# A Mamba and expert-layer kernel: another order for the end of the last chunk, expert weights gathered in four parts, expert chunks in a written order

## The chip, the cores and the metric

The kernel runs on one core of one Trainium2 chip. The metric is the device time of one execution in microseconds (us); the time of a kernel is the median of its runs. The core has five engines that run side by side: TensorE (PE, matrix products; PEld is its loading of weights), VectorE (DVE), ScalarE (ACT), GpSimd (POOL) and SyncE (SP, which here only issues DMAs). Each engine works through its own list of instructions in order and waits on semaphores for the others.

## What is computed

The input is one image of 64 x 64 positions with 256 channels, float32. Two layers are applied, each with residuals:

```
# layer 0
x = x + conv_attention(group_norm(x, 32 groups))
#   1x1, 3x3 and 5x5 convolutions give q, k, v; depthwise 3x3; 8 heads;
#   softmax attention over the 4096 positions; 1x1 projection
# layer 1, t = the 4096 tokens of 256 channels
n = layer_norm(t)
m = mamba_forward(n) + mamba_backward(n)     # inner width 512, state 16, scan over 4096 tokens
h = layer_norm(m) * ln_g + ln_b
t = t + m + leaky_relu(h @ w1.T + b1, 0.01) @ w2.T + b2
# mixture of 8 experts (256 -> 512 -> 256) on n = layer_norm(t)
logits = mean(n, tokens) @ Wr + br           # one routing for the whole sample
two experts by weight -> top_i, softmax of their weights -> top_w
y = sum_k top_w[k] * (gelu(n @ W1[e_k] + b1[e_k]) @ W2[e_k] + b2[e_k])
t = t + layer_norm(y + n) * gamma + beta
```

As the routing hangs on the mean over all tokens, no expert's weights can be fetched before the last token has left the Mamba stage.

## The kernel before, in words

The program has four phases, one behind the other: `conv_phase`, `attention_phase`, `mamba_phase` and `expert_phase`. The tokens are worked in 8 chunks (`NCH`) of 512 tokens (`N`). A tile of a chunk is 128 partitions x 2 x 512: the 256 channels lie in `CT` = 2 groups on the partitions, the tokens in the free direction. A mean over channels is therefore a matmul with the constant `mean_mat`. `P` is 128, `FT` is 4 (512 inner channels by 128).

**The Mamba phase.** Its loop runs over 512 slots: 16 passes (8 chunks forward, 8 backward) of 32 slots. In each slot `recur` issues on DVE one scan over 128 x 1024 elements (L1907, 2.35 us) and one product with C (L1912, 1.22 us), while ACT makes the decays (L1884) and POOL the inputs dbx (L1894) of slots to come. The order of the instructions on every engine is written out by hand: the whole loop stands in `tc.manual_schedule(engines=ORDERED)`, so an engine gets its instructions in the order in which the Python code makes them. Other work is dealt into the slots as generators, piece by piece: each `yield` ends a piece, and `step` runs a generator to its next `yield`.

- `tail(c)` (L1539) is the work on a finished chunk: LayerNorm of `m` (`layer_norm`, L101 to L150, its last product L149 on POOL), the leaky-ReLU MLP, the residual, the LayerNorm whose result goes to `u2d` in HBM, and the sum over tokens `usum` (L1583) that the routing needs. It has 39 pieces, one dealt per slot (L2039). With one piece per slot the tail of chunk 6 does not end within the last pass: its rest is drained in `ending()`.
- `ahead()` (L1687) prepares the end of the last chunk within the last pass. It makes `wc` and the two 128 x 128 matrices `near` and `far`, by which the last output projection is made with its mean taken off, and `b1p` and `b1c` (L1709 to L1714): the bias of the MLP with `ln_b` folded in, and 0.01 times that.
- `ending()` (L1768) finishes the last chunk: the last parts of the projections (`plain`, L1735; `close`), the LayerNorm by small matmuls (`rstd_of`: sums of squares of 128 tokens each into one column, then a power on POOL; `spread`: the four values per partition laid on diagonals, L1763, and spread over the partitions by a matmul, L1766), up projections with leaky ReLU (L1809 to L1811), down projections (L1820), the last residual, the LayerNorm of the expert layer, scores and `router()` (L2045).

`router` leaves `rows_of` (L2065), the rows of the two chosen experts in HBM, and `tw` (L2082), their two weights. Its scratch (`slab`) lies in the tile `win`, which lies where later the gathered weights go.

**The expert phase.** Four indirect DMAs on POOL's queue (L2105) gather the two experts' weights, two halves of a row of 2054 floats for each partition: W1, W2, b1, b2. DVE scales W2 by the expert's weight and takes its mean over channels off (L2113 to L2125). Then for each chunk: load `u` (normed tokens) and `x` (residual) on SP's queue (L2137, L2139), eight groups of two up matmuls with a gelu on ACT each (L2165, L2168), sixteen down matmuls (L2175), `r` = their sum plus bias plus `u` (L2179). A float32 matmul of 512 columns stands in the trace as two records of 0.429 us at full clock. `finish(c)` normalizes `r` while the next chunk runs, one piece behind each gelu: Square (L131), the two matmuls of the sum of squares (L122), four small DMAs with POOL's power between them, product (L149), gamma and beta (L2150), residual (L2153), store (L2154). The last chunk uses `fast_norm` (L154 to L179), in the manner of `rstd_of` and `spread`. This phase stands outside the written order: the framework's scheduler places the instructions. `pmm`, `po` and `pln` are the PSUM pools of the up matmuls, the down matmuls (two buffers) and the LayerNorms.

## Time and profile before

| what | value |
|---|---|
| median of 3 runs | 4116.2 us (4112.8, 4116.2, 4122.62) |
| the profiled execution | 4114.68 us, span 4112.9 us, mean granted clock 0.919 |
| busy: PE, DVE, ACT, POOL | 87%, 85%, 65%, 45% of the span |
| last pass of the Mamba phase | to about 3806 us |
| `ending()` and router | 3806 to 3850 us |
| first gather issued, first up matmul | 3851.05, 3859.03 us |
| experts, one chunk | 29.17 us, 68 PE records |
| last chunk's first matmul | 4065.07 us |
| last down matmul, last store issued | about 4094.4, 4106.47 us |

Times count from the start of the span, so a place in the program is named by its microsecond. A line of the timeline has start, duration, engine, line of the kernel, operation, result and operands, shape, and, where the engine stood idle just before, for how long and what released it. The granted clock is the share of TensorE's full speed that the throttle let through: at 0.5 a matmul record takes twice as long.

### The profile page before, as it was taken

The page shows a single profiled execution, that of the slowest core. Times are in us where ns is not written, and L with a number is a line of the kernel's source. Part 1 is how long each engine was busy: PE and PEld are TensorE (multiplying, and loading weights), DVE is VectorE, ACT ScalarE, POOL GpSimd, SP SyncE. Part 2 cuts the span into 40 slices and gives each one's busy share as a digit, 9 for nine tenths or more (in the row PEclk, how much of TensorE's full clock was granted, in tenths as well). Part 3 has the DMA queues.
Part 4 walks back from the last instruction along what each step waited for, and adds up shares of the span by engine and source line. Part 5 has one row for each costly group of instructions (what it writes and reads, how often), then busy time and mean ns, then how long its engine had stood idle before and what let it go on. Part 6 is the DMA issues. An engine that isn't in the chain of part 4 may idle for free. (4 is left out here: it accounts for less than half of the span.)

```text
span 4112.9 us, 43197 instructions
## 1 busy us (share of the span) xinstructions
PE 3584.9 (87%) x14772; PEld 1175.0 (29%) x14772; DVE 3499.8 (85%) x2908; ACT 2666.2 (65%) x4146; POOL 1839.2 (45%) x1283
## 2 busy tenths in 40 slices
PE   6769888999999999997888888888888888876898
PEld 2324332222222222222222222222222222222343
DVE  8998877989888888877899999999999999999211
ACT  1111226988887888875777778778787778775222
POOL 3020000000000000002888889888888989987000
PEclk9889998999999999998888988998989899988899
DMA  6222215223322322214333344343433334432221
GB/s 208 93 98 96 81 58 157 52 60 65 66 62 55 65 63 57 58 39 138 116 103 121 114 137 139 101 141 106 135 106 127 121 124 120 132 118 80 75 68 35
DMA packets 164051, 399.92 MB, mean 97 GB/s; under 512 B 36981, under 2 KB 45941, under 8 KB 163566
## 3 DMA queue, kind: packets, MB, share of 16 engines
q1 hardware_dynamic: 139198, 312.65, 24.0%
q0 software_dynamic: 24624, 84.43, 8.8%
q8 instruction: 118, 1.93, 0.2%
q14 instruction: 111, 0.91, 0.1%
HBM read 268.16 MB, written 79.56 MB: 85 GB/s over the span
## 5 line engine op out<-in xcount | busy, mean ns | idle before, releaser
L1894 POOL TENSOR_TENSOR dbx<-dtxr,b 128x1024 f32<-128x1024 f32 x512 | 1203.7, 2362 | 197.3 <-DMA dtxr<-dtd 91.3
L1046 ACT ACTIVATE e<-sc 128x1024 f32<-128x1024 f32 x1024 | 993.7, 1023 | 172.0 <-PE sc L1039 147.1
L1907 DVE TENSOR_TENSOR_SCAN da<-da,state,dbx 128x1024 f32<-128x1024 f32 x432 | 1013.9, 2347 | 14.6 <-ACT da L1884 7.2
L956 DVE TENSOR_TENSOR s<-s,e 128x1024 f32<-128x1024 f32 x768 | 880.4, 1216 | 25.0 <-ACT e L1046 24.3
L1884 ACT ACTIVATE da<-dtr,aneg 128x512 f32<-128x512 f32 x1024 | 708.0, 691 | 32.6 <-DMA dtr<-dtd 3.1
L1039 PE MATMUL sc<-q,kS 32*128 32x512 f32 x4096 | 651.9, 648 | 18.6 <-ACT e L1046 13.9
L1912 DVE TENSOR_TENSOR h<-da,c 128x1024 f32<-128x1024 f32 x432 | 529.1, 1225 | 33.1 <-PE y L1947 1.3
L963 PE MATMUL av<-e,vT 128*32 128x512 f32 x4096 | 553.6, 611 | 0.0
L979 POOL DMA_DIRECT2D s<-s x94 | 81.6, 879 | 946.5 <-DVE s L956 856.1
L1947 PE MATMUL y<-h,sel 128*32 128x512 f32 x2048 | 376.1, 664 | 91.6 <-DVE h L1912 66.4
L464 PE MATMUL cv<-v,u 128*128 128x512 f32 x928 | 414.6, 607 | 28.8 <-DVE v L288 13.3
L1039 PEld LDWEIGHTS sc<-q,kS 32*128 32x128 f32 x4096 | 211.4, 185 | 460.7 <-issue 253.1
L1341 PE MATMUL mm<-u,win 128*128 128x512 f32 x464 | 253.6, 697 | 77.6 <-ACT z L1448 25.8
L464 PEld LDWEIGHTS cv<-v,u 128*128 128x128 f32 x928 | 179.4, 195 | 261.7 <-issue 227.8
L562 DVE SCALAR_TENSOR_TENSOR acc<-pad,wdw_s,acc 128x768 f32<-128x768 f32 (+1 forms) x192 | 236.0, 1234 | 19.9 <-ACT acc L555 14.2
L1938 ACT COPY state<-da 128x2 f32<-128x2 f32 x431 | 67.9, 158 | 265.6 <-DVE h L1912 264.7
L143 POOL TENSOR_TENSOR ln_few<-ln_few,minus_half 128x4 f32<-128x4 f32 x29 | 37.4, 1291 | 400.5 <-DMA ln_few<-ln_row 265.4
L1387 PE MATMUL mm<-xp,taps 128*128 128x512 f32 x480 | 213.0, 596 | 0.1
L956 DVE TENSOR_TENSOR s<-e 128x1024 f32<-128x1024 f32 x128 | 151.9, 1217 | 59.5 <-ACT e L1046 59.3
L1907 DVE TENSOR_TENSOR_SCAN h<-da,state,dbx 128x1024 f32<-128x1024 f32 x80 | 187.5, 2344 | 10.6 <-ACT state L1938 9.9
L963 PEld LDWEIGHTS av<-e,vT 128*32 128x32 f32 x4096 | 81.4, 108 | 397.0 <-issue 389.2
L1917 POOL TENSOR_TENSOR h<-h,c 128x1024 f32<-128x1024 f32 x80 | 188.6, 2357 | 1.0 <-ACT state L1938 1.0
(382 smaller groups left out, 3922.1 us busy)
## 6 DMA issues: line engine op xcount, KB each, us to landing
dtr<-dtd SPq DMA_DIRECT2D x128, 512.0 KB
dtxr<-dtd SPq DMA_DIRECT2D x128, 512.0 KB
s<-s POOLq DMA_DIRECT2D x94, 512.0 KB, 6.0
b<-bcd SPq DMA_DIRECT2D x64, 256.0 KB
c<-bcd SPq DMA_DIRECT2D x64, 256.0 KB
dtd<-dt SPq DMA_DIRECT2D x64, 256.0 KB
dtd<-few SPq DMA_DIRECT2D x64, 256.0 KB
u<-uv SPq DMA_DIRECT2D x24, 640.0 KB
```

What stands on the lines that cost most here:

```text
L464: nc.tensor.matmul(rows4(ps), u[:, dy, P * ci : P * ci + P], v[:, dy : dy + HR, ci, :], start=dy + ci == 0, stop=dy == k - 1 and ci == CT - 1,
L562: nc.vector.scalar_tensor_tensor(o, src, w_ap, o, ALU.mult, ALU.add)
L956: nc.vector.tensor_tensor(z, x, y, ALU.add)
L963: nc.tensor.matmul(g.av[32 * h : 32 * h + 32, :], vT[:, kb, P * t + 32 * h : P * t + 32 * h + 32], es[h // 2][:, h % 2, :], start=kb == 0, ...
L1039: nc.tensor.matmul(ps[h // 2][:, h % 2, :], kS[r, t, P * kb : P * kb + P], q_t[r, t, :], start=True, stop=True,)
L1046: nc.scalar.activation(e, ps[i], AF.Exp)
L1341: nc.tensor.matmul(ps, win[d][:, t, P * e : P * e + P], u[:, t, ::-1] if d else u[:, t, :], start=t == 0, stop=t == CT - 1,)
L1884: nc.scalar.activation(da[:, v, :], dts[i, e, j][0][:, v, :], AF.Exp, scale=aneg[i % 2][:, a : a + 1])
L1894: nc.gpsimd.tensor_tensor(u, dts[i, e, j][1], bcs[i, k][0][:, None, :].to_broadcast([P, 2, N]), ALU.mult)
L1907: nc.vector.tensor_tensor_scan(das[n].rearrange("p v n -> p (v n)"), da.rearrange("p v n -> p (v n)"), u.rearrange("p v n -> p (v n)"), st ...
L1912: nc.vector.tensor_tensor(h, da, bcs[i, k][1][:, None, :].to_broadcast([P, 2, N]), ALU.mult)
L1947: nc.tensor.matmul(ys[i, e][32 * j : 32 * j + 32, :], cx.sel, hs[n + j // 2][:, j % 2, :], start=False, stop=k == SQ - 1,)
```

## The change

- `fast_norm` goes. In its place two small functions serve both the end of the Mamba phase and the last expert chunk: `deviations` (sums of squares, reading, power) and `spread` (diagonals and their matmul). Both can work on a part of the columns.
- `ahead()` yields between the small matmuls of `b1p` and their DVE readers; slot 17 joins the list of slots in which `ahead()` gets a step.
- In slots 4, 6 and 7 of the last pass two tail pieces are dealt in place of one.
- `ending()`: Square ahead of the copy; the deviations get a PSUM tile of their own; the spread comes before the rest of the tail is drained; all four up projections come before the first down projection; of the scores only the first pair of matmuls comes before the deviations; the scratch of the router moves to another pool; the store of `u2` goes to ACT's queue.
- The row of an expert's weights becomes W1, b1 | W2, b2, padding (two halves of 1028 floats). Four separate tiles are gathered, in the order W1 and b1 of both experts, then W2 and b2 of both. The gathers then wait for `rows_of` and no longer for `tw`.
- The first `u` is loaded on SP's queue ahead of the gathers. Each chunk's `x` and the next chunk's `u` are issued on ACT's queue behind the fourth gelu.
- The chunk loop stands in the written order. The LayerNorms of chunks 0 to 6 are called with `halves=True`: DVE adds the two channel groups first, and one matmul sums.
- `last_chunk` works the last chunk's down projections in four quarters (two halves of 256 columns, two channel groups) and normalizes and stores each half by itself; beta is added to `x` on ACT.

```diff
-EXPERT_ROW = 2 * FF + 4 * C + FT + CT
+EXPERT_ROW = 2 * (2 * FF + FT)
...
+def deviations(cx, few, ps, sq, cols=range(N // P)):
+    nc, at = cx.nc, slice(cols[0], cols[-1] + 1)
+    for j in cols:
         for t in range(CT):
             nc.tensor.matmul(
-                ps[:, j : j + 1], dst[:, t, P * j : P * j + P], cx.mean_mat[:, 0:1], start=t == 0, stop=t == CT - 1
+                ps[:, j : j + 1], sq[:, t, P * j : P * j + P], cx.mean_mat[:, 0:1], start=t == 0, stop=t == CT - 1
             )
-    nc.scalar.activation(few, ps[:, 0 : N // P], AF.Identity, bias=cx.eps)
-    nc.gpsimd.tensor_tensor(few, few, cx.minus_half, ALU.pow)
-    diag = pool.tile([P, N], FP, name="ln_rstd", tag="ln_rstd", bufs=1)
-    for j in range(N // P):
-        nc.vector.tensor_scalar(diag[:, P * j : P * j + P], cx.ident, few[:, j : j + 1], float(C), ALU.mult, ALU.mult)
-    ps = new_psum()
-    nc.tensor.matmul(ps, cx.mean_mat, diag, start=True, stop=True)
-    nc.vector.tensor_tensor(dst, xc, ps[:, None, :].to_broadcast([P, CT, N]), ALU.mult)
+    nc.scalar.activation(few[:, at], ps[:, at], AF.Identity, bias=cx.eps)
+    nc.gpsimd.tensor_tensor(few[:, at], few[:, at], cx.minus_half[:, at], ALU.pow)
+def spread(cx, ps, diag, few, cols=range(N // P)):
+    for j in cols:
+        cx.nc.vector.tensor_scalar(
+            diag[:, P * j : P * j + P], cx.ident, few[:, j : j + 1], float(C), ALU.mult, ALU.mult
+        )
+    at = slice(P * cols[0], P * cols[-1] + P)
+    cx.nc.tensor.matmul(ps[:, at], cx.mean_mat, diag[:, at], start=True, stop=True)
...
+            yield
             nc.vector.tensor_tensor(b1p, ps[:, 0:FT], cx.col("b1", 0, FT), ALU.add)
             nc.vector.tensor_scalar(b1c, b1p, 0.01, None, ALU.mult)
...
+                nc.scalar.activation(sq[:, co, :], centred[co], AF.Square)
                 nc.vector.tensor_copy(xc[:, co, :], centred[co])
-                nc.scalar.activation(sq[:, co, :], centred[co], AF.Square)
             plain(1, 1)
             few = tl.tile([P, N // P], FP, name="ln_few", tag="ln_few")
-            rstd_of(few, wide[:, 1, :], sq)
+            deviations(cx, few, mm_psum(), sq)
...
             plain(1, 2, 3)
             plain(0, 3)
-            for t in tails:
-                drain(t)
-            spread(wide[:, 1, :], few)
+            rs = mm_psum()
+            spread(cx, rs, bcp.tile([P, N], FP, name="diag", tag="b"), few)
...
+            for t in tails:
+                drain(t)
             pair = pda.tile([P, 2, N], FP, name="pv", tag="da")
-            halves = []
-            for f in range(FT):
-                if f % 2 == 0:
-                    a = tl.tile([P, 2, N], FP, name="a1a", tag=("ln_xc", "a1b")[f // 2])
-                    halves.append(a)
-                pv = mm_psum() if f < 2 else pair[:, f - 2, :]
+            pv = [None] * FT
+            halves = [tl.tile([P, 2, N], FP, name="a1a", tag=tag) for tag in ("ln_xc", "a1b")]
+            def up_proj(f):
...
+            for f in range(2):
+                up_proj(f)
+                leaky(f)
+            for f in range(2, FT):
+                up_proj(f)
+            for f in range(2):
+                down_proj(f)
+            for f in range(2, FT):
+                leaky(f)
+            for f in range(2, FT):
+                down_proj(f)
...
+            score(0)
             few2 = tl.tile([P, N // P], FP, name="ln_few", tag="ln_few")
-            rstd_of(few2, pz, u2)
+            deviations(cx, few2, mm_psum(), u2)
+            for j in range(1, N // P):
+                score(j)
+            slab_of[0], used[0] = up.tile([P, 2, N], FP, name="slab", tag="dbx")[:, 0, :], 0
...
+            nc.scalar.dma_start(out=u2d[c], in_=u2)
+        end, used, slab_of = {}, [2 * P], [win[0][:, 1, :]]
...
-                if i == 2 * NCH - 1 and at in (4, 5, 6, 7, 10, 11, 12, 13, 15, 19, 21, 23, 25, 27, 28, 29, 30):
+                if i == 2 * NCH - 1 and at in (4, 5, 6, 7, 10, 11, 12, 13, 15, 17, 19, 21, 23, 25, 27, 28, 29, 30):
                     last = last or ahead()
                     step(last)
-                if tails and (i == 2 * NCH - 1 or at not in FULL[needs[0]]):
-                    needs[0] = next(tails[0], None)
-                    if needs[0] is None:
-                        tails.pop(0)
-                        needs[0] = "PE"
+                for _ in range(1 + (i == 2 * NCH - 1 and at in (4, 6, 7))):
+                    if tails and (i == 2 * NCH - 1 or at not in FULL[needs[0]]):
+                        needs[0] = next(tails[0], None)
+                        if needs[0] is None:
+                            tails.pop(0)
+                            needs[0] = "PE"
...
+        def load(c, queue):
+            u = io.tile([P, CT, N], FP, name="u", tag="u")
+            queue.dma_start(out=u, in_=u2d[c])
+            return u
         tw = cx.tw
-        HALF = EXPERT_ROW // 2
-        w1s, w2s, b1s = [], [], []
-        b2s = one.tile([P, CT], FP, name="b2s")
-        for k in range(2):
-            ew = one.tile([P, EXPERT_ROW], FP, name=f"ew{k}")
-            for h in range(2):
+        u_next = load(0, nc.sync)
+        ew = [[one.tile([P, EXPERT_ROW // 2], FP, name=f"ew{k}{h}") for h in range(2)] for k in range(2)]
+        for h in range(2):
+            for k in range(2):
                 nc.gpsimd.indirect_dma_start(
-                    out=ew[:, HALF * h : HALF * h + HALF], out_offset=None,
-                    in_=experts.rearrange("r (h c) -> (r h) c", h=2),
+                    out=ew[k][h], out_offset=None, in_=experts.rearrange("r (h c) -> (r h) c", h=2),
                     in_offset=bass.IndirectOffsetOnAxis(ap=cx.rows_of[:, k, h : h + 1], axis=0),
                 )
-            a, b, c = 2 * FF, 2 * FF + 4 * C, 2 * FF + 4 * C + FT
+        w1s = [ew[k][0][:, 0 : 2 * FF].rearrange("p (t f) -> p t f", t=CT) for k in range(2)]
+        b1s = [ew[k][0][:, 2 * FF : 2 * FF + FT] for k in range(2)]
+        w2s, b2s = [], one.tile([P, CT], FP, name="b2s")
...
-            new = lambda: pln.tile([P, N], FP, name="ln", tag="ln")
-            if c < NCH - 1:
-                yield from layer_norm(cx, tl, new, r, o, centred=True)
-            else:
-                fast_norm(cx, tl, new, r, o, centred=True)
+            yield from layer_norm(
+                cx, tl, lambda: pln.tile([P, N], FP, name="ln", tag="ln"), r, o, centred=True, halves=True
+            )
...
+        def last_chunk(u, x, h):
+            c, both = NCH - 1, (range(0, N // P // 2), range(N // P // 2, N // P))
             r = tl.tile([P, CT, N], FP, name="r", tag="r")
+            sq = io.tile([P, CT, N], FP, name="sq", tag="u")
+            o = io.tile([P, CT, N], FP, name="o", tag="o")
+            few = tl.tile([P, N // P], FP, name="ln_few", tag="ln_few", bufs=1)
+            diag = tl.tile([P, N], FP, name="diag", tag="ln_rstd", bufs=1)
+            stat = [pln.tile([P, N], FP, name="ln", tag="ln") for _ in range(2)]
+            for t in range(CT):
+                nc.scalar.activation(x[:, t, :], x[:, t, :], AF.Identity, bias=cx.col("beta", t))
+            def part(half, co):
+                cols = slice(P * half[0], P * half[-1] + P)
+                ps = po.tile([P, N], FP, name="o", tag="o")[:, 0 : N // 2]
+                down_proj(ps, co, h, cols)
+                nc.vector.scalar_tensor_tensor(
+                    r[:, co, cols], ps, b2s[:, co : co + 1], u[:, co, cols], ALU.add, ALU.add
+                )
+                nc.scalar.activation(sq[:, co, cols], r[:, co, cols], AF.Square)
+            def write(half):
+                cols = slice(P * half[0], P * half[-1] + P)
+                for t in range(CT):
+                    nc.vector.scalar_tensor_tensor(
+                        o[:, t, cols], r[:, t, cols], cx.col("gamma", t), stat[1][:, cols], ALU.mult, ALU.mult
+                    )
+                nc.vector.tensor_tensor(o[:, :, cols], o[:, :, cols], x[:, :, cols], ALU.add)
+                nc.sync.dma_start(
+                    out=outT[:, N * c + cols.start : N * c + cols.stop].rearrange("(t p) n -> p t n", p=P),
+                    in_=o[:, :, cols],
+                )
             for co in range(CT):
-                ps = po.tile([P, N], FP, name="o", tag="o")
+                part(both[0], co)
+            part(both[1], 0)
+            deviations(cx, few, stat[0], sq, both[0])
+            part(both[1], 1)
+            spread(cx, stat[1], diag, few, both[0])
+            deviations(cx, few, stat[0], sq, both[1])
+            write(both[0])
+            spread(cx, stat[1], diag, few, both[1])
+            write(both[1])
+        behind = None
+        with tc.manual_schedule(engines=ORDERED):
+            for c in range(NCH):
+                u, h = u_next, hp.tile([P, 2, FT, N], FP, name="h", tag="h")
                 for k in range(2):
                     for f in range(FT):
-                        nc.tensor.matmul(
-                            ps, w2s[k][:, f, P * co : P * co + P], h[:, k, f, :],
-                            start=k + f == 0, stop=k == 1 and f == FT - 1,
-                        )
-                nc.vector.scalar_tensor_tensor(
-                    r[:, co, :], ps, b2s[:, co : co + 1], u[:, co, :], ALU.add, ALU.add
-                )
-            drain(behind)
-            behind = finish(c, r, x)
-        drain(behind)
+                        ps = pmm.tile([P, N], FP, name="mm", tag="mm")
+                        for t in range(CT):
+                            nc.tensor.matmul(
+                                ps, w1s[k][:, t, P * f : P * f + P], u[:, t, :], start=t == 0, stop=t == CT - 1
+                            )
+                        nc.scalar.activation(h[:, k, f, :], ps, AF.Gelu, bias=b1s[k][:, f : f + 1])
+                        step(behind)
+                    if k == 0:
+                        x = io.tile([P, CT, N], FP, name="x", tag="x")
+                        nc.scalar.dma_start(out=x, in_=x2d[c])
+                        if c < NCH - 1:
+                            u_next = load(c + 1, nc.scalar)
+                drain(behind)
+                if c == NCH - 1:
+                    last_chunk(u, x, h)
+                    break
+                r = tl.tile([P, CT, N], FP, name="r", tag="r")
+                for co in range(CT):
+                    ps = po.tile([P, N], FP, name="o", tag="o")
+                    down_proj(ps, co, h, slice(0, N))
+                    nc.vector.scalar_tensor_tensor(
+                        r[:, co, :], ps, b2s[:, co : co + 1], u[:, co, :], ALU.add, ALU.add
+                    )
+                behind = finish(c, r, x)
```

## The prediction

> **What bounds the kernel now.** I read the page's busy shares and its forty slices first, then the stretches after 3700 us, where the edits lie, by windows, and inside them by the timeline with its releasers.
>
> ```profile
> span 4112.9 us, 43197 instructions
> PE 3584.9 (87%) x14772; PEld 1175.0 (29%) x14772; DVE 3499.8 (85%) x2908; ACT 2666.2 (65%) x4146; POOL 1839.2 (45%) x1283
> ...
> 3840.00:3860.00 20.00, 7.72 (x37) 5.50 (x37) 4.56 (x23) 2.53 (x6) 4.95 (x5) 0.58 0.43 146
> 3880.00:3900.00 20.00, 20.00 (x48) 8.89 (x47) 1.50 (x2) 4.37 (x6) 0.00 (x0) 1.00 0.08 26
> ```
>
> The windows' columns are PE, PEld, DVE, ACT and POOL busy, granted clock, DMA share, GB/s. The shares are averages over stages that differ: in the last Mamba pass (to about 3806) DVE runs scan behind scan and every us on it counts. From 3807 to 3867 nothing is full; a chain of waits sets the time, mostly at half clock. In the experts PE is full, and nothing but fewer matmul records helps. From 4094.4 a chain again.
>
> ```profile
> 3744.07 0.16 DVE L1713 TENSOR_TENSOR win<-mm,small 128x4 f32<-128x4 f32 x1 [1.35 <-PE mm L1709]
> 3744.27 0.98 DVE L1714 TENSOR_SCALAR b1c<-win 128x4 f32<-128x4 f32 x1
> 3764.28 0.99 PE L1571 MATMUL tl<-a1a,w2s 128*128 128x512 f32 x1 [2.36 <-DVE m L1576]
> 3815.99 1.22 DVE L1583 TENSOR_REDUCE usum<-u 128x2 f32<-128x1024 f32 x1 [6.18 <-POOL u L149]
> 3817.12 0.86 DVE L1763 TENSOR_SCALAR diag<-ident,ln_few 128x128 f32<-128x128 f32 x4
> 3827.04 1.98 PE L1809 MATMUL pv<-hn_end,w1s 128*128 128x512 f32 x4 [1.56 <-DVE a1a L1811]
> 3851.05 1.09 POOL L2105 DMA_INDIRECT ew<-in_experts,rows_of  x1 [6.80 <-DVE diag L1763]
> 3866.11 0.75 DVE L2113 TENSOR_SCALAR w2k<-ew,tw 128x1024 f32<-128x1024 f32 x1 [1.71 <-DMA ew<-in_experts,rows_of]
> 4070.22 1.88 PE L122 MATMUL ln<-o,mean_mat 128*128 128x512 f32 x4
> 4072.19 0.68 ACT L136 ACTIVATE ln_rstd<-ln,eps 1x512 f32<-1x512 f32 x1 [1.08 <-PE ln L122]
> 4082.51 1.22 DVE L149 TENSOR_TENSOR o<-r,ln_rstd 128x1024 f32<-128x1024 f32 x1 [16.48 <-DMA ln_rstd<-ln_inv]
> 4105.22 1.22 DVE L2153 TENSOR_TENSOR o<-o,x 128x1024 f32<-128x1024 f32 x1
> ```
>
> To be seen: DVE stops for b1p in the last pass; the diagonals (pow of `few` done at 3813.65) stand 3.5 us behind the reduce of tail(6); the gathers wait for DVE and the fourth, landing at 3866.05, holds up PE; each expert LayerNorm costs PE four records.
>
> **The change, part by part.** Line numbers are those of before. Gains are positive.
>
> (1) *Last pass.* The new yield puts a slot (some 3.6 us) between the 16 small matmuls and their DVE reader, so the 1.35 stall goes, and of the 0.98 all but the 0.16 of its neighbour: +2.17. The doubled slots let tail(6) finish inside the pass, so L1583 (1.22) comes before the last scan, on a full DVE: -1.22. POOL's `hn` (3711.44, 2.36) and its ACT readers come a slot earlier among the dbx and decay instructions that feed the scans; no row shows what that does. Bounds: nothing (the pieces before were all absorbed) and three slots at 0.69, the stall of DVE at 3770.70, so -2.1. I take 0, since neither engine is full (dbx 2.36 and decay 1.42 in 3.6). Part: +0.95 (-1.1 to +2.2).
>
> (2) *ending() to `rows_of`.* Square ahead of the copy: 3808.98 becomes 3808.25, +0.73. `few` no longer shares the tile of the plain sums, which waited from 3812.21 to 3812.61: +0.40. The diagonals no longer wait for L1583, but the spread (3818.04) then waits for PE's plain records, done at 3816.99 and now at 3815.9: together about +2.1 from this stretch. All up matmuls before the first down: the 1.56 stall and its weight load go, +1.65. Six of the eight score matmuls go behind the deviations, which started at 3840.88 though their Square had ended at 3839.91: +0.85 of these 0.97, as two scores stay ahead. Sum +4.6, with the pass +5.5 (low 3, high 6.8). What is late next: PE at half clock.
>
> (3) *Gathers.* They waited for the last write of `tw` (ends 3850.11) and now for `rows_of` (3848.23): +1.88, so the first is issued at S = 3851.05 - 5.5 - 1.9 = 3843.6. Before, it landed 7.85 later and the fourth 11.1 after its issue, while six u and x loads (3.1 MB) and 2.1 MB of gathers filled the DMA engines from 3852 to 3866. Now one u load has come before, the others are issued after the fourth gelu. Landing without company: the page's other 512 KB transfers on POOL's queue take 6.0. Upper bound as before (7.85, 11.1), lower 4.3 for the first (1.09 issue, 1.3 us of 526 KB at 410 GB/s, and 2 us of latency, an estimate from the 128 KB row's 2.5). I take 6.0: first at S+6.0, fourth at S+9.9 with the same spacing of issues. PE does 10 records before the b2s matmul: 4.5 us at half clock (as 3859.03 to 3863.5) are 5.25 of them, the rest take 0.429: S+12.5. The b2s operand, 1.1 after the fourth landing, is ready at S+11.0 and no longer the last. With b2s (0.58) and one matmul (0.86), ten up matmuls are left at S+14.0 = 3857.6; before, they were left at 3867.57. Gain up to here 10.0 (6.5 with landings as before, 11.7 with the fast ones).
>
> (4) *Seven LayerNorms.* One DVE add and one matmul for two matmuls: 2 records of 0.429 less, 7 x 0.86 = +6.0. Cover of the add: Square, behind the second gelu, ends at T+5.4 (T: chunk start), the add (0.7) at T+6.15, its matmul stands after four groups at T+6.86. Slack 0.7. If the add is late, PE stops for the difference; no row excludes it: 0 to +6.0, I take 6.0.
>
> (5) *Last chunk.* Chunk 6's rstd copy stands in ACT's written order behind the fifth gelu, T+10.35, where before it was at 4072.19 = T+7.12. From it to L149 it took 10.32 (four small DMAs and POOL's pow), so L149 falls at T+20.7 and the last add at T+24.2 (3.55 later, as 4082.51 to 4086.05). The first quarter's `r` stands on DVE behind that add, and PE's third quarter needs its PSUM buffer. PE finishes 34 records at T+14.6 and two quarters of 16 records of 256 columns at 0.2145 (half of 0.429, an estimate) at T+21.45; it then waits to T+24.7: -3.2. After the gap I charge half clock for 3.5 us, as from 3764.56 to 3768 behind a gap of 2.36: -1.7 (0 if not; gaps of 1.56 and 2.20 kept the clock).
> [...]
> Behind the last matmul before: 12.0 (4094.4 to 4106.44). After: r 0.48, Square 0.45, deviations 0.94, few 0.26, pow 1.01, diagonals 0.43, spread 1.2, two products at 0.42 and an add of 0.65, with some 0.1 between: 7.1. The first half's deviations (0.94) now stand on PE among the quarters; the first half's spread and write lie beside Square and pow. The last transfer is half as large: +0.7. So 12.0 - 7.1 - 0.94 + 0.7 = +4.7, less 4.9: -0.2 (-1.5 to +4.7).
>
> Sum: 10.0 + 6.0 - 0.2 = 15.8. The profiled execution took 4114.7 (span 4112.9), 1.5 under the median of 4116.2: 4098.9, so 4099.
>
> **Rivals.**
> (a) *Gathers no faster.* They landed late for another reason than the loads: gain 6.5 instead of 10.0, 4102.5. For: the first landed 7.85 after its issue although only two loads stood ahead of it. Against: a DMA share of 1.0 all through.
> (b) *Last chunk without a stall*, L149 coming before the second quarter ends: 4.9 back, 4094. Against: the 10.32 chain is four transfers long.
> (c) *Doubled slots starve the scans*, POOL behind by a `hn` product of 2.36 at two of three slots: 4.7 lost, 4103.5. For: no slack of a whole product there.
> (d) *The written order stops PE in every chunk*, at the matmul of the halves' sum: slower. Place: L115 to L120. With an add late by 0.7 nothing is lost; 15.8/7 = 2.3 us of wait in each of seven chunks bring the time to no change, and at 2.36 the half clock joins: 4.1 each, 28.7 of which 15.8 were gained, 4128. It decides where Square ends 3 us later than T+5.4. Against: ACT is busy 4.37 of 20 and DVE 1.50 of 20 in a steady window, so both come in time.
> (e) *The gap of the last chunk keeps the full clock*, as those of 1.56 and 2.20 did: 1.7 back, 4097.2. Against: the gap of 2.36 did not. [...]
>
> **How the numbers follow.** Forecast 0.36, (a) 0.14, (b) 0.14, (c) 0.08, (e) 0.10: all faster, 0.82. (d) 0.18: smaller waits that eat the gain 0.08 (same), the full one 0.10 (slower). About 0.2%, 8 us, is what a measurement of this kernel can tell from no change. Range: low 4091 (fast landings and no stall, 4114.7 - 11.7 - 6.0 - 4.7 = 4092.3, and a us of scatter), high 4110 (landings as before, half of the LayerNorm gain, a starved scan, nothing from the last chunk: 4114.7 - 6.5 - 3.0 + 4.7 = 4109.9); outside lie (d)'s cases for the most part.
>
> **What would show it.** Right: no DVE stall at b1c; L1583 ahead of the last scan; first gather near 3843.6 and landings of about 6; ten up matmuls left near 3858; chunk period 28.3 instead of 29.17; PE idle 3.2 in the last chunk before the third quarter, half clock behind it; 7 us from the last matmul to the last add. Wrong: PE idle before each LayerNorm matmul, gathers landing after 8 and more, new DVE stalls at the doubled slots, or no gap in the last chunk.

## The result

| | median | fastest to slowest of 20 runs |
|---|---|---|
| before | 4119.69 us | 4109.88 to 4135.72 |
| changed | 4108.01 us | 4100.43 to 4117.78 |

The medians lie 11.7 us apart. The ratio of changed to before is 0.9968, 95% interval 0.9959 to 0.9976, which stands for 13 us less (10 to 17). The forecast was faster, 4099, range 4091 to 4110. The time lies inside, near its upper end.

The two profiled executions seem to contradict this: spans of 4112.9 and 4112.1 us. The difference lies ahead of the change. The last pass's last close (DVE's `xc`) is at 3806.34 before and at 3820.51 after, and 11.7 of these 14.2 us had gathered when the last pass began, in code that is the same in both. Another execution of the changed kernel had that close at 3806.43. So in what follows only stretches are compared, and each starts at a landmark of its own execution.

The page of the changed kernel, its span and its busy shares:

```profile
span 4112.1 us, 43244 instructions
PE 3586.2 (87%) x14792; PEld 1183.0 (29%) x14792; DVE 3503.9 (85%) x2919; ACT 2667.8 (65%) x4152; POOL 1836.6 (45%) x1284
```

And a window of a steady expert chunk (PE, PEld, DVE, ACT, POOL busy, clock, DMA share, GB/s):

```profile
3880.00:3900.00 20.00, 20.00 (x48) 8.88 (x47) 2.19 (x3) 3.58 (x5) 0.00 (x0) 1.00 0.00 0
```

The shares say nothing of the change, as they said nothing of its place before. PE still fills an expert chunk, with the LayerNorm's add on DVE beside it. The timeline of the changed kernel shows where the time went (places are this execution's own):

```profile
3761.01 0.69 DVE L1952 TENSOR_TENSOR xc<-y,z 128x512 f32<-128x512 f32 x1 [1.25 <-PE y L1943]
3765.14 0.15 DVE L1712 TENSOR_TENSOR win<-mm,small 128x4 f32<-128x4 f32 x1
3765.33 1.08 DVE L1713 TENSOR_SCALAR b1c<-win 128x4 f32<-128x4 f32 x1
3778.49 1.22 DVE L129 TENSOR_TENSOR ln_xc<-m,tl 128x1024 f32<-128x1024 f32 x1 [1.14 <-PE tl L122]
3814.55 1.22 DVE L1581 TENSOR_REDUCE usum<-u 128x2 f32<-128x1024 f32 x1
3827.25 0.87 DVE L169 TENSOR_SCALAR diag<-ident,ln_few 128x128 f32<-128x128 f32 x4 [2.65 <-POOL ln_few L163]
3852.50 0.20 ACT L1846 ACTIVATE slab<-tl 128x32 f32<-128x32 f32 x1 [2.14 <-PE tl L1832]
3857.67 1.09 POOL L2105 DMA_INDIRECT ew<-in_experts,rows_of  x1 [6.22 <-DVE slab L2072]
3862.36 6.87 PE L2209 MATMUL mm<-u,ew 128*128 128x512 f32 x10 [0.75 <-DMA ew<-in_experts,rows_of]
4070.24 1.02 PE L119 MATMUL ln<-ln_both,mean_mat 128*128 128x512 f32 x2
4073.59 0.66 ACT L136 ACTIVATE ln_rstd<-ln,eps 1x512 f32<-1x512 f32 x1
4083.87 1.22 DVE L149 TENSOR_TENSOR o<-r,ln_rstd 128x1024 f32<-128x1024 f32 x1 [14.51 <-DMA ln_rstd<-ln_inv]
4087.84 5.41 PE L2151 MATMUL o<-h,w2k 128*128 128x256 f32 x16 [2.81 <-DVE r L2173]
4103.94 0.69 DVE L2184 TENSOR_TENSOR o<-o,x 128x512 f32<-128x512 f32 x1
```

To be seen, from the top: DVE no longer waits for b1p, but waits for `y` and for a mean, which it did not do there before, and makes the reduce of `usum` inside the pass. The diagonals follow the power at once. The scores' reading (L1846) is 1.0 behind the power's end at 3851.45 and is what the routing now waits for. The gathers land early. The LayerNorm matmul of a chunk has two records. In the last chunk PE stands for 2.81 before the third quarter.

All profiled executions, the experiments too, in us. The last pass is counted from the last close of the pass before to its own last close; the other columns behind that last close. `gap` is PE's wait in the last chunk, and behind it whether the clock fell to one half. The experiments from after_again to scores were timed once each, so they are read by these stretches and not by their whole time.

| kernel | last pass | index of the rows | first up matmul | last add ends | gap, clock |
|---|---|---|---|---|---|
| before | 116.6 | 41.7 | 52.7 | 300.1 | none |
| changed | 119.1 | 36.1 | 41.9 | 284.1 | 2.81, half |
| after_again | 119.1 | 36.1 | 41.7 | 284.6 | 2.52, half |
| single | 115.4 | 39.7 | 45.2 | 288.0 | 2.52, half |
| two | 115.4 | 37.6 | 43.3 | 285.8 | 2.65, half |
| nostall | 120.4 | 36.0 | 41.6 | 279.9 | none |
| loads | 120.5 | 36.0 | 41.6 | 285.2 | 2.68, full |
| loads2 | 118.9 | 36.2 | 45.4 | 291.9 | 2.82, half |
| warm | 119.0 | 36.1 | 41.8 | 282.0 | 2.66, full |
| warm_b2s | 120.5 | 36.0 | 41.8 | 281.3 | 2.81, half |
| whole | 120.5 | 36.0 | 41.8 | 290.7 | 2.13, full |
| scores | 120.5 | 36.8 | 42.5 | 285.8 | 2.94, half |
| best | 119.6 | 36.6 | 42.2 | 276.5 | none |
| best2 | 115.1 | 37.3 | 42.9 | 277.7 | none |

From the pass to the end of the span the change gives 116.6 + 300.1 + 6.5 = 423.2 before (6.5 is what follows the last add) and 119.1 + 284.1 + 7.5 = 410.7 after: 12.5 us, in agreement with the timed ratio.

### The profile page after: what moved, and what is told of

Its sections match the earlier page's. It is cut to its first block, busy times and chain, and to the rows that moved or that the text cites. A ratio compares the mean times of both kernels' runs of the same rounds, so it can differ in the third digit from the quotient of the medians.

```text
span 4112.1 us, 43244 instructions
## 1 busy us (share of the span) xinstructions
PE 3586.2 (87%) x14792; PEld 1183.0 (29%) x14792; DVE 3503.9 (85%) x2919; ACT 2667.8 (65%) x4152; POOL 1836.6 (45%) x1284
## 5 line engine op out<-in xcount | busy, mean ns | idle before, releaser
L462 PE MATMUL cv<-v,u 128*128 128x512 f32 x928 | 414.9, 607 | 28.7 <-DVE v L286 13.3
L560 DVE SCALAR_TENSOR_TENSOR acc<-pad,wdw_s,acc 128x768 f32<-128x768 f32 (+1 forms) x192 | 236.0, 1234 | 19.9 <-ACT acc L553 14.2
L1903 DVE TENSOR_TENSOR_SCAN h<-da,state,dbx 128x1024 f32<-128x1024 f32 x80 | 187.5, 2344 | 13.0 <-ACT state L1934 11.7
```

The lines of the kernel that those rows point to most:

```text
L462: nc.tensor.matmul(rows4(ps), u[:, dy, P * ci : P * ci + P], v[:, dy : dy + HR, ci, :], start=dy + ci == 0, stop=dy == k - 1 and ci == CT - 1,
L560: nc.vector.scalar_tensor_tensor(o, src, w_ap, o, ALU.mult, ALU.add)
L1903: nc.vector.tensor_tensor_scan(das[n].rearrange("p v n -> p (v n)"), da.rearrange("p v n -> p (v n)"), u.rearrange("p v n -> p (v n)"), st ...
```

## The experiments

### The same kernel again

No edit.

> The changed kernel once more, for the scatter of each stretch. If the stretches are properties of the program: from the scan behind the first close of the last pass to its last close again 118.5 us (before 116.0), from there to the index of the rows 36.1 (before 41.7), to the b2s matmul 49.2, the last chunk from its first up matmul to its last add 41.3 with the gap of 2.8 in front of the third quarter, each within 0.3 us. If the two new waits of the last pass (1.25 and 1.14 us) were chance: the last pass near 116.5.

The last pass took 119.1 again, and the waits for `y` and the mean were 1.25 and 1.14 again. (The first two expectations count the pass 0.6 later, behind that close's own product: 118.5 and 116.0 there are 119.1 and 116.6 in the table.) So a loss in the pass belongs to the program, but its size is not fixed. Seven of the later runs have the same last pass: in loads2 and warm it took 118.9 and 119.0, in the five others 120.4 to 120.5, with a wait for `y` of 2.9 in place of 1.25. In these five, half clock lies on the four records of the tail in front of that `y` (3.64 us in nostall, 1.98 in the changed kernel). Of the kernel before there is one profile, so its own scatter is not known. Behind the close everything repeats within 0.5 us, but for where half clock falls (below).

### One tail piece per slot

```diff
-for _ in range(1 + (i == 2 * NCH - 1 and at in (4, 6, 7))):
+for _ in range(1 + (i == 2 * NCH - 1 and at in ())):
```

> Undoes one part: one tail piece per slot in slots 4, 6 and 7 too, all else as changed. Theory A, the doubled slots bunch PE's work so that DVE waits for y and for the mean, and buy nothing, since the drain in ending() now stands behind hn: the last pass gets shorter by the reduce (1.22) and by most of the new waits (some 2 us), to about 115.2 us, and the index of the rows stays 36.1 +- 0.5 behind the last close. Rival B, the doubling pays in ending(): the last pass loses only the reduce (117.3), and the product on POOL and the reduce of tail(6), back in ending(), put the index of the rows 2 us or more later, so nothing is won.

Both theories hold half. The pass became 3.7 shorter, 1.22 of it the reduce and the rest the new waits. But the index of the rows came 3.6 later, and the sum of pass and rest is 403.4, against 403.3 and 403.8. The doubled slots buy in `ending()` what they cost in the pass. The timeline of single shows how:

```profile
3812.46 1.01 POOL L163 TENSOR_TENSOR ln_few<-ln_few,minus_half 128x4 f32<-128x4 f32 x1 [12.06 <-ACT ln_few L162]
3813.44 2.34 POOL L149 TENSOR_TENSOR u<-ln_xc,ln_rstd 128x1024 f32<-128x1024 f32 x1
3813.50 2.94 DVE L169 TENSOR_SCALAR diag<-ident,ln_few 128x128 f32<-128x128 f32 x4 [2.65 <-POOL ln_few L163]
```

The four diagonals take 0.87 us in the changed kernel and 2.94 here, and they end 0.66 behind POOL's product (3815.78), which had begun just ahead of them. Three of the four take 0.65, so the first of them stood as long as POOL worked. Drained behind `hn` in the code, the product starts on POOL as soon as the power is done, and so just beside the diagonals. That is 2.1 of the 3.6. The other 1.5 is clock, nearly all: the second deviations (L159) took 3.56 instead of 2.14, because half clock began 0.4 us behind their start and not 2 us behind it.

### Two doubled slots

```diff
-for _ in range(1 + (i == 2 * NCH - 1 and at in (4, 6, 7))):
+for _ in range(1 + (i == 2 * NCH - 1 and at in (4, 6))):
```

> Two doubled slots (4 and 6), not three and not none. In the changed kernel the tail's large matmuls fall on odd slots, where ahead() puts its own; with two they fall on even slots, and the reduce of tail(6) comes behind the last product of the pass, into the wait for y. Theory, the third doubling costs by this collision: the last pass falls from 119.1 to about 115.5 us (measured from the second-to-last pass's last close to the last close), the waits for y and for the mean go, and the index of the rows stays 36.1 behind the close, since POOL's product is done before the diagonals; in all 3.6 us less. Rival, any doubling bunches PE's work, or the reduce delays the close: the pass takes 117.5 or more.

The pass fell to 115.4, as the theory had it, the mean came in time, and `hn` stayed 8.9 behind the close (single 11.0). The reduce stands in front of the close, as meant, which then waits only 0.19. But the index came 1.5 later, again with deviations of 3.56 at half clock. Pass and rest together: 401.2, 2.3 less than the changed kernel's mean of 403.5. That the pass stays at 115.4 is not settled: in best, which has the same slots, it took 119.6, with 1.75 and 3.05 us of waiting for `y`. There the plain sums in front of the last `y` ran at half clock (2.08 for two records that took 1.13 in two), and the windows of best show it:

```profile
3802.00:3804.00 2.00, 0.87 (x8) 0.83 0.00 0
3804.00:3806.00 2.00, 1.76 (x4) 0.50 0.57 227
3806.00:3808.00 2.00, 2.00 (x5) 0.50 0.09 35
3808.00:3810.00 2.00, 2.00 (x4) 0.50 0.00 0
```

(Columns: PE busy, clock, DMA share, GB/s.) PE is not the bound of this pass, but it is near enough that a stretch at half clock in front of a close decides.

### The last chunk without the LayerNorm in its way

```diff
-                        step(behind)
+                        if c < NCH - 1 or 4 * k + f < 6:
+                            step(behind)
...
-                drain(behind)
+                if c < NCH - 1:
+                    drain(behind)
...
             for co in range(CT):
                 part(both[0], co)
+            drain(behind)
             part(both[1], 0)
```

> Last chunk only: the last pieces of chunk 6's LayerNorm (product, gamma and beta, residual, store) are written behind the second quarter instead of among the up matmuls, so that the first two r stand ahead of them on DVE. Theory, the gap is PE waiting for r behind that LayerNorm, and it halves the clock: the gap of 2.8 goes, the clock stays full, and the last chunk from first up matmul to last add takes 41.26 - 2.8 - 1.7 = 36.8 us. Rival: the 3.5 us of DVE work only moves and holds up the third quarter's r and the first half's deviations instead: PE waits there, some 2 us, and the chunk takes 39 or more.

The gap went and the clock stayed full: PE ran three quarters in one stretch, and from the close to the last add it took 279.9 in place of 284.1 and 284.6. The theory's 4.5 were 4.4. In the timeline of nostall:

```profile
4070.52 10.52 PE L2151 MATMUL o<-h,w2k 128*128 128x256 f32 x48
...
4077.63 0.48 DVE L2173 SCALAR_TENSOR_TENSOR r<-o,b2s,u 128x256 f32<-128x256 f32 x1 [2.97 <-PE o L2151]
4078.03 1.22 DVE L149 TENSOR_TENSOR o<-r,ln_rstd 128x1024 f32<-128x1024 f32 x1
```

### Loads beside the gathers

In loads, five x and u loads are issued on ACT's queue in the lines behind the gathers; from chunk 3 on, x and u are then fetched two chunks ahead, behind the eighth gelu.

```diff
+        xs, us = {}, {0: u_next}
+        for c in range(3):
+            if c:
+                us[c] = load(c, nc.scalar)
+            xs[c] = io.tile([P, CT, N], FP, name="x", tag="x")
+            nc.scalar.dma_start(out=xs[c], in_=x2d[c])
```

> The x and u loads of the first three chunks (five of 512 KB, 2.6 MB) are issued on ACT's queue directly behind the gathers' issue, about where the kernel before had them, not behind the fourth gelu. Theory, the early landing of the gathers (4.6 us for the first, before 7.85) comes from their having the DMA engines alone: the first up matmul falls from 41.85 behind the last close to about 45, the b2s matmul from 49.2 to 53 or later. Rival, the gathers are limited by their own descriptors and were late before for the order of the parts: both stay within 1 us.

The first up matmul stayed at 41.6, but the run says nothing on the question. These lines stand outside the written order, and the loads were placed earlier: the trace has them issued from 13.3 to 2.6 us ahead of the first gather, not beside it. In loads2 they stand in a written order behind a copy of the index:

```diff
+        hold = one.tile([P, 2, 2], mybir.dt.uint32, name="hold")
+        with tc.manual_schedule(engines=ORDERED):
+            nc.sync.dma_start(out=hold, in_=cx.rows_of)
+            for c in range(3):
+                if c:
+                    us[c] = load(c, nc.sync)
+                xs[c] = io.tile([P, CT, N], FP, name="x", tag="x")
+                nc.sync.dma_start(out=xs[c], in_=x2d[c])
```

> As the loads run, but the five x and u loads wait on SP's queue for the index of the rows (a 2 KB copy of it stands ahead of them), so that they are issued with the gathers and not long before. Theory, the DMA engines are shared and the loads hold up the gathers: first landing 7 us or more after its issue in place of 4.6, first up matmul 44 or later behind the close, b2s matmul 52 or later (49.5 without). Rival, the gathers are bound by their own descriptors: both within 1 us of the changed kernel's.

Now the gathers landed late, as before the change. What the trace answers on the gathers' line in the changed kernel, then in loads2, and the first up matmul in the timeline of loads2:

```profile
DMA to landing us min/median/max: 4.6/6.1/6.5
```

```profile
DMA to landing us min/median/max: 8.2/10.8/12.6
```

```profile
3851.45 6.76 PE L2218 MATMUL mm<-u,ew 128*128 128x512 f32 x10 [4.27 <-DMA ew<-in_experts,rows_of]
```

Before it was 7.7/9.0/11.0; the smallest is 4.4 to 4.7 in all twelve profiles without such loads beside the gathers. The first up matmul comes at 45.4 instead of 41.7 to 41.9, the b2s matmul at 54.9 instead of 49.2 to 49.8, and the last add 7.5 us later. So contention with the loads is what made the gathers late, and to move the loads behind the fourth gelu was a main part of the gain.

### TensorE kept busy before the experts

```diff
+            idle = mm_psum()
+            for _ in range(3):
+                nc.tensor.matmul(idle, cx.mean_mat, x2c[:, 0, :], start=True, stop=True)
             router(cx, slab, pl)
```

> Three matmuls of 512 columns whose result is not used are added on TensorE between the routing's logits and the spread, where it stood idle for 4.9 us at half clock. Theory, half clock behind a sparse stretch costs the first up matmuls 0.43 us a record: they start at full clock and the first ten records take 4.3 instead of 6.9 us. But the b2s matmul behind them waits for the fourth gather: its place stays at 49.5 +- 0.5 and nothing is won. Rival, the gathers land in time and all of the 2.5 us is won.

The result of the three matmuls is not used. The up matmuls ran at full clock from the first on (timeline of warm; in the changed kernel ten records took 6.87):

```profile
3851.91 5.47 PE L1853 MATMUL mm<-x2c,mean_mat 128*128 128x512 f32 x6
3859.61 6.28 PE L2212 MATMUL mm<-u,ew 128*128 128x512 f32 x14 [1.26 <-DMA ew<-in_experts,rows_of]
```

But the b2s matmul, now behind fourteen records, waited 2.16 us for its operand, so that chunk 1 starts only 1.0 earlier (first gelu at 74.1; 74.8 and 75.4 in the changed kernel). Neither theory was exact: some was won, not all. The rest of the 2.4 at the last add is the clock, which did not fall behind the gap of the last chunk.

In warm_b2s the b2s matmul stands behind the up matmuls of chunk 0:

```diff
-        ps = pln.tile([P, N], FP, name="ln", tag="ln")
-        for t in range(CT):
-            nc.tensor.matmul(ps[:, 0:1], cx.mean_mat, b2s[:, t : t + 1], start=t == 0, stop=t == CT - 1)
-        nc.vector.tensor_tensor(b2s, b2s, ps[:, 0:1].to_broadcast([P, CT]), ALU.subtract)
...
+                if c == 0:
+                    ps = pln.tile([P, N], FP, name="ln", tag="ln")
+                    for t in range(CT):
+                        nc.tensor.matmul(ps[:, 0:1], cx.mean_mat, b2s[:, t : t + 1], start=t == 0, stop=t == CT - 1)
+                    nc.vector.tensor_tensor(b2s, b2s, ps[:, 0:1].to_broadcast([P, CT]), ALU.subtract)
                 drain(behind)
```

> As the warm run, and the b2s matmul, which needs the fourth gather, stands behind all the up matmuls of chunk 0 instead of behind the fifth. Theory, the wait for the fourth gather then stands on nobody's way: the end of the last chunk moves from 284.4 behind the last close to about 281 (2.5 for the clock, 0.5 for the wait). Rival, the down matmuls then wait for the second expert's scaled weights: nothing is won.

All 32 records of chunk 0's up matmuls ran in one stretch of 14.0 us, chunk 1's first gelu came at 71.7, 3.4 earlier than the changed kernel's mean, and the last add at 281.3, 3.1 earlier. The theory had 3.

### The LayerNorms by two matmuls, and the scores ahead

In whole, `halves=True` is left off; in scores, all score matmuls stand ahead of the deviations.

```diff
-                cx, tl, lambda: pln.tile([P, N], FP, name="ln", tag="ln"), r, o, centred=True, halves=True
+                cx, tl, lambda: pln.tile([P, N], FP, name="ln", tag="ln"), r, o, centred=True
```

> One part undone: the LayerNorms of chunks 0 to 6 sum the two channel groups by two matmuls again, with no DVE add; the written order stays. Theory, the add costs nothing on the path and saves two records of 0.429 in each of seven chunks, and by the piece that it adds it is also what makes chunk 6's LayerNorm late: the chunk period goes from 28.32 to 29.18, so the last chunk starts 5.15 later, but the row of chunk 6 goes out one gelu earlier, the gap of 2.8 before the third quarter goes, and the last chunk takes about 37.6 us instead of 41.3. The last add comes 1.5 later behind the last close than the changed kernel's 284.4, about 286. Rival, the gap is there with either form: 290.

Here my theory fell and the rival held: the gap is there in either form (2.13), and the last add came 6.3 later. The row's copy (L136) went out 7.7 behind the chunk's first gelu, in the changed kernel 8.3: hardly earlier, because in either form it stands in ACT's written order behind a gelu that waits for PE. Before, the framework's order let it follow its matmul at once (4072.19, the matmul done at 4072.10). So the added piece is not what makes chunk 6's LayerNorm late. That the written order does, with one piece dealt per gelu, is read from these rows; no run takes it away alone. The chunk period became 29.46, not 29.18: in the timeline of whole, the LayerNorm's matmuls stand where Square isn't quite done.

```profile
4061.65 0.30 PEld L122 LDWEIGHTS ln<-o,mean_mat 128*128 128x128 f32 x2 [0.83 <-ACT o L131]
4061.66 1.98 PE L122 MATMUL ln<-o,mean_mat 128*128 128x512 f32 x4
```

```diff
-            score(0)
+            for j in range(N // P):
+                score(j)
             few2 = tl.tile([P, N // P], FP, name="ln_few", tag="ln_few")
             deviations(cx, few2, mm_psum(), u2)
-            for j in range(1, N // P):
-                score(j)
```

> One part undone: all eight score matmuls stand ahead of the deviations again. Theory, in the changed kernel the six moved ones take 2.6 us at half clock and end 1.0 behind the power that they were to run beside, so that the move wins nothing: the index of the rows comes at 35.9 to 36.3 behind the last close, as now (36.1). Rival, the move is worth the 0.85 that I had put on it: 36.9 or later.

The index came at 36.8, between the two: the move is worth 0.7. With it, the deviations run before half clock begins (2.14 for them; in scores 2.79), but the scores behind them run at half clock (2.60 for twelve records; 1.73 for fourteen in scores) and end last.

### Put together

best has the edits of two, nostall and warm_b2s. best2 also makes b1c on ScalarE:

```diff
-            nc.vector.tensor_scalar(b1c, b1p, 0.01, None, ALU.mult)
+            nc.scalar.activation(b1c, b1p, AF.Identity, scale=0.01)
```

> Four edits of earlier runs together: two doubled slots, chunk 6's LayerNorm behind the second quarter, the three idle matmuls, the b2s matmul behind the up matmuls. Theory, they lie in different stretches and add up: last pass 115.4 us (119.1 in the changed kernel), last close to last add 284.4 - 4.4 - 3.1 + 0 to 1.5 for where half clock falls in the routing = 276.9 to 278.4; in all 9.5 to 11 us less than the changed kernel and 21 to 23 less than the kernel before, 0.9945 to 0.995 of it. Rival, what is won in one stretch is lost behind it, as happened to single and two: less than 6 us.

> As best, and the 128x4 product b1c, which took DVE 0.98 us before and 1.08 as changed, is made on ScalarE. Theory, the DVE instruction ends with POOL's product that runs beside it (the two wait for each other), so it goes from DVE's path: the last pass is 0.9 shorter than best's, about 114.5 us. Rival, ScalarE has to wait for DVE's b1p, and the decays behind it come late: the pass stays at 115.4 or gets longer.

| kernel | median | ratio to before, 95% interval |
|---|---|---|
| best | 4098.93 us | 0.9948 (0.9934 to 0.9962) |
| best2 | 4094.54 us | 0.9934 (0.9914 to 0.9955) |

Behind the close the gains add up as expected (276.5 and 277.7). The last pass of best did not, for the half clock shown above. In best2 it took 115.1, where 114.5 was expected. b1c takes 0.20 on ScalarE. The fair comparison is with two, which has the same 0.45 and 0.19 of waits at its closes: best2's pass is 0.36 shorter. The product is gone from DVE, but 0.69 of what that freed went into a new wait of DVE for PE's projection, so most of the 0.9 was not won. The interval of best2 lies wholly below the changed kernel's (0.9959 to 0.9976), so it beats both kernels; best's overlaps that one by 0.0003. Best and best2 overlap each other, so which of these two is the faster isn't shown.

## Why the prediction was right, and which steps were off

By its own steps, in us gained, for the profiled execution:

| step | forecast | measured |
|---|---|---|
| (1) last pass | +0.95 | -2.5 |
| (2) ending() to the index of the rows | +4.6 | +5.65 |
| (3) gathers, to ten up matmuls left | +4.5 | +5.1 |
| (4) seven LayerNorms | +6.0 | +6.0 |
| (5) last chunk and end | -0.2 | -1.75 |
| sum | 15.8 | 12.5 |

(3) is the forecast of 10.0 without the 5.5 of (1) and (2).

**(1) failed.** "Of the 0.98 all but the 0.16 of its neighbour" was no stall of b1p's: b1c still takes 1.08. And the doubled slots, bounded by "nothing" and -2.1 and taken at 0, cost about 2.5, beyond that bound (single's pass is 3.7 shorter, of which the reduce is 1.2): they put the tail's matmuls into slots where PE has others ahead of `y` and of the mean. The row that gave the bound, DVE's stall of 0.69 at 3770.70, waits for PE's `y` in the trace, so it named the late engine. That neither POOL nor ACT is full was no argument; PE was late. The chance lay with rival (c), which had the place but the wrong engine.

**(2)** was larger at `hn` (4.0 in place of 2.1) since without the wait for `few` PE also kept the full clock: 0.67, 0.50, 0.50 and 0.62 in the four us from 3812 before, 1.00 in the four from 3826 after, and the four records of the plain sums took 1.96 in place of 3.52. The clock stayed full there in all thirteen profiles of the new order, and `hn` came at 8.9 in all but single; that the missing wait is the reason is inferred, as no run restores it alone. It was smaller at the scores (-0.2 in place of 0.85): half clock began 5.7 us behind the last down projection's result and not 7.1 as before, and took it back. Run scores gives the move itself 0.7.

**(3)** held: 1.88 for the index in place of `tw` (the first gather went from 44.7 to 37.2 behind the close, 7.55 in all, of which 5.65 is (2)). The first landing was sized too long, 4.6 in place of 6.0; the lower bound of 4.3 was nearer. Its cause, the loads, is shown by loads2. Rival (a) is out.

**(4)** held to the record: from chunk 1 to chunk 7 the starts lie 28.32 apart, 29.18 before, and PE does not wait for the add. By the last chunk's start six of the seven are done, and they gave 5.15. Rival (d) is out.

**(5)** The gap was forecast at 3.2, by L149 at 20.7 behind the chunk's start and the third quarter released at 24.7. It was 2.81, with L149 at 20.5 and the quarter at 24.5. The half clock behind it was forecast at 3.5 us: it lasted 3.4. The end behind the last matmul, 7.1, was 7.0. What was wrong is "the last transfer is half as large: +0.7": from the last add to the end of the span it took 6.5 before and 6.7 to 7.7 in the thirteen profiles with a half store. The half store has as many packets as the whole one, 256, of 1 KB in place of 2 KB, and its data were done 2.58 behind the add in the changed kernel (2.3 to 2.7 in all thirteen), before 2.56: nothing was won there. The stretch after the data took 3.9 before and 4.0 to 5.0 after. Why isn't known; there is one profile of before. Rival (b) is out: the gap stands in all ten executions without nostall's edit.

So the sum was too large by 3.3: (1) missed by 3.45 and (5) by 1.55, and (2) and (3) gave 1.65 more than forecast. That these errors partly cancel is luck. Most of the remaining distance from 4099 to 4108 is the reference: the sum was made against 4114.7, and the median of before over 20 runs is 4119.7.

Rival (e), the clock surviving the gap, came true in three executions of ten (table: loads, warm and whole, at gaps of 2.68, 2.66 and 2.13), and not in the profiled one.

## What to carry to other kernels

Work that is off the critical path by its engine's share can still cost when it is dealt into a full pass: ask of every moved piece which matmul it now stands in front of, and at which clock. A written order makes each engine wait in the order of the code, so a small copy written behind a large instruction of another chain inherits its wait: here 3 us on ACT became a gap on PE two engines further on. Before a latency is blamed on a transfer, look at what else is in flight: the same gathers landed in 4.6 or in 8.2 us by the loads beside them alone.

## What was unexpected in the hardware

**The clock moved on a fixed grid.** In all fourteen traces every stretch at half clock, but the last that the end of the span cuts, lasts a whole multiple of 3.413 us. Before there are 83 of them and in the changed kernel 92, of 3.413 to 27.31 us, and in both traces every change of the clock lies within 0.01 us of one grid of 3.413. The length of a gap alone did not decide what came behind it: one of 2.52 was followed by half clock in two executions, one of 2.68 in another was not. Laid on the grid of its own trace, each of the seven gaps behind which the clock fell left 2.32 to 2.82 us of a single step of 3.413 without a matmul (2.34 of the step from 4085.50 to 4088.91 in the changed kernel), and the next step ran at half clock; the three others left at most 1.75 in one step. Windows of the changed kernel behind its gap, and then of warm (PE busy, clock, DMA share, GB/s):

```profile
4086.00:4087.00 1.00, 0.00 (x0) 1.00 0.00 0
4087.00:4088.00 1.00, 0.16 (x1) 1.00 0.00 0
4088.00:4089.00 1.00, 1.00 (x5) 0.96 0.64 252
4089.00:4090.00 1.00, 1.00 (x4) 0.50 0.71 272
4091.00:4092.00 1.00, 1.00 (x4) 0.50 0.00 0
```

```profile
4083.00:4084.00 1.00, 0.00 (x0) 1.00 0.00 0
4085.00:4086.00 1.00, 1.00 (x7) 1.00 0.99 389
4086.00:4087.00 1.00, 1.00 (x7) 1.00 0.16 59
```

The last chunk, from its first up matmul to the last add, took 41.1 to 41.7 us where the clock fell behind the gap and 39.5 to 39.9 where it did not. DVE's wait for `y` in front of the last close is 0.19 in two and 3.05 in best, with the same edit in the pass.

**A DVE product waited for POOL.** A product of 128x4 by a constant took 0.98 before, 1.08 after and 0.20 on ScalarE; the same form took 0.16 on DVE with POOL idle (`off`, the second row below, from the timeline of whole). Beside POOL it ends with POOL's product: before at 3745.25, POOL (from 3742.87, 2.36) at 3745.23; after at 3766.41, POOL at 3766.38:

```profile
3764.04 2.34 POOL L1890 TENSOR_TENSOR dbx<-dtxr,b 128x1024 f32<-128x1024 f32 x1 [3.17 <-DVE da L1903]
3855.47 0.16 DVE L2126 TENSOR_SCALAR off<-off 128x4 f32<-128x4 f32 x1
```

The diagonals of single show it with 2.94 in place of 0.87. DVE's scans and POOL's dbx run side by side all through the pass and keep their 2.35 and 2.36, and b1p's add took 0.15 beside the same product of POOL, so not every DVE instruction waited there. In the rows above POOL had begun first each time. Elsewhere other forms were longer too, and POOL's product as well: in the changed kernel a DVE sum of 128x512 (`dt`, L1623) took 2.72 at 1942.44, beside a product of POOL, and 0.69 at 1946.26, and the product of POOL that began at 1946.38, while that second sum ran, took 2.77 in place of 2.36. A busy time in the profile can thus be a wait, and I had read it as one of another kind.
